# Column scores of two heads in one bank pair, with one exponential for both, once the row maxima are done

## The chip, the cores and the metric

The kernel runs on one core of one Trainium2 chip. The metric is device time in microseconds. Shown of the kernel before are three runs, with a median of 933.51 us (931.16 to 935.1), and one profiled execution, which took 931.65 us.

The core has a matrix engine (TensorE, PE in the profile), which multiplies out of SBUF and writes into PSUM, and four more engines with queues of their own: VectorE (DVE), ScalarE (ACT), GpSimd (POOL) and SyncE (SP), which here only issues DMAs. Each engine works through its own queue in order; they wait for one another by semaphores. PSUM has eight banks, and one bank holds 512 float32 columns on 128 partitions.

## The reference, cut to what matters

Input x is 2 x 2048 x 256. It is normalised by rows, and three things are added up: x itself, attention over the normalised rows, and a linear map of them that stands for a Fourier transform, a sparse product and the inverse transform.

```python
xn = layernorm(x)                                  # rows of 256
q = rope((xn @ wq).reshape(B, S, 16, 16))          # 16 heads of 16
k = rope((xn @ wk).reshape(B, S, 4, 16))           # 4 key heads, each used by 4 query heads
v = (xn @ wv).reshape(B, S, 4, 16)
scores = einsum('bshd,bthd->bhst', q, k) / 4       # causal: t <= s
out = softmax(scores) @ v
y = x + out @ wo + real(ifft(fft(xn) @ w)) + bias
```

All is float32. The head size is 16, so the 2 x 16 x 2048 x 2048 scores, half of them masked, are by far the most work.

## The kernel before, in words

The sequence is cut in blocks of 512 rows (SB), four in each of the two batches, eight blocks n in all. A unit u = (n, g) is one block of query rows with four of the 16 heads. There are 32 units, and the last, 31, belongs to the last block. Queries and keys are split in three bfloat16 parts each and stacked along the contraction (112 rows, and 3 more for the maximum), so that bfloat16 products give float32 scores.

Each unit passes two stages.

- *Row scores* (`maxima`, from line 593): scores with query rows on the partitions, only to find each row's maximum. Two heads (`head(0)`, `head(1)`) write the two banks of one tile `sm` of 2 x 512 columns from the pool `ps_s`; one VectorE maximum at line 636 reads both. The pool has two such tiles: four banks. `parts` then splits the negative maximum in three bfloat16 parts, and `spread` turns them (tile `ps_m`) and copies them (tile `mt`) into the last three rows of the stacked queries (lines 671 to 678, the last a DMA that ScalarE issues).
- *Column scores* (`scores`, line 691): scores with keys on the partitions, 128 at a time. A step is one such group of 128 keys for the four heads. Each head writes its own bank `st` of the pool `ps_st` (three banks), with the maximum already subtracted through the three extra rows. ScalarE then takes the exponential into half of an SBUF tile `es`, which holds a pair of heads (line 726). On the four steps of the diagonal the first columns drop out: 512, 384, 256 and 128 columns are left. There GpSimd masks the triangle of the pair (line 729).

`values` (line 744) multiplies the four exponentials of a step with v into the one bank `av`, at line 757; a column of ones beside v gives the sum of the exponentials. At the end of a unit `take` copies `av` into `avs` (line 768). For most units the division is done by DMA and GpSimd; for the last two it goes through TensorE (`divide`, line 819, tile `ps_a`) and `turn_back` (line 839). `output` (line 872) multiplies with `wo_sb` and the spectral matrix `mff` into a bank `po`, also from `ps_st`; the last block's outputs are begun early, without their last term, and finished at the end.

The order is written out by a planner, the loop from line 1069 on. It keeps a clock per engine, and prices for each piece (`use`, line 114; `through_bank`, line 143: TensorE fills a bank, another engine empties it). Among the pieces that could start it picks one: B is the next head's column scores, V the next step's values, A the next row scores, S a spread, F and M other pieces with and without a due time. The pieces of all queues are issued in the order in which it picks them. `ring` and `used` count the buffers of each pool, so that it knows when one comes free. `a_done` counts the row maxima issued, of `a_list` in all. TensorE's chain of work is L155 (`product`, one score or weight product as four quarters of 32 partitions), L757 (values), and L631 and L627 (row scores on the diagonal, with their mask).

Of the kernel before, what the change touches and what calls it, by code (L numbers as in the profile page):

```python
# [10 lines left out]
F32 = mybir.dt.float32  # L11
BF16 = mybir.dt.bfloat16
AF = mybir.ActivationFunctionType
# [4 lines left out]
P = 128  # L18
# [5 lines left out]
def tile_attn_plus_spectral_ffn(  # L24
# [29 lines left out]
    nc = tc.nc  # L54

    _, S, D = x.shape
# [8 lines left out]
    SB = 512  # L65
    NI = SB // P
    NJ = S // SB
    NK = D // P
    SCALE = DH ** -0.5
# [6 lines left out]
    ES = 8  # L76
# [3 lines left out]
    at_block = {bj: n for n, bj in enumerate(blocks)}  # L80
# [4 lines left out]
    ps_st = ctx.enter_context(tc.tile_pool(name="ps_st", bufs=3, space=PSUM))  # L85
    ps_s = ctx.enter_context(tc.tile_pool(name="ps_s", bufs=2, space=PSUM))
# [6 lines left out]
    ring, used = {}, {}  # L93
# [6 lines left out]
    def take_slot(tag):  # L100
        used[tag] += 1
        return used[tag] - 1
# [11 lines left out]
    def use(eng, us, needs=(), gives=()):  # L114
        clock[eng] = max(clock[eng], ready(needs)) + us
        for k in gives:
            there[k] = clock[eng] + LATE[eng]
# [25 lines left out]
    def through_bank(us, needs, eng, eng_us, gives, eng_needs=()):  # L143

        k = take_slot("st")
        use("pe", us, (*needs, ("st", k - ring["st"])), [("ps", k)])
        use(eng, eng_us, (("ps", k), *eng_needs), [("st", k), *gives])
# [220 lines left out]
    xnT, va, kst, qst = {}, {}, {}, {}  # L368
# [319 lines left out]

    es, av, es_slot = {}, {}, {}

    def scores(u, t, h):
        n, g = units[u]
        b, j = blocks[n]
        kb = kst[at_block[b, t // NI]]
        kc = (t % NI) * P
        lo = max(0, t - j * NI) * P
        pr, e = divmod(h, 2)
        if e == 0:
            es[u, t, pr] = work.tile([P, 2, SB], F32, tag="es", bufs=ES, name=f"es{u}_{t}_{pr}")
            es_slot[u, t, pr] = take_slot("es")  # L700
        ps = ps_st.tile([P, SB], F32, tag="st", name=f"st{u}_{t}_{h}")
        keys, rows = kb[0:KA, h, kc : kc + P], qst[n, g][0:KA, h, :]
        wd = SB - lo
        through_bank(
            (wd + 32 * (lo > 0 or t == 0 == j)) * 4.28e-4,
            [("mt", n, g), ("kst", at_block[b, t // NI])],
            "act", 0.06 + wd * 8.4e-4, [("es", u, t, pr)],
            [("es", es_slot[u, t, pr] - ES)],
        )
        diagonal = t >= j * NI  # L710
        if diagonal and j == 0:


            for q in range(0, P, QD):
                to, at = ps[q : q + QD, :], lo + q
                nc.tensor.matmul(  # L716
                    to[:, lo : at + QD], ident_h[:, q : q + QD], mask_t[:, : q + QD],
                    start=True, stop=True, skip_group_check=True,
                )
                nc.tensor.matmul(  # L720
                    to[:, at:], keys[:, q : q + QD], rows[:, at:],
                    start=False, stop=True, skip_group_check=True,
                )
        else:
            product(ps[:, lo:], keys, rows[:, lo:], True, True)
        nc.scalar.activation(es[u, t, pr][:, e, lo:], ps[:, lo:], AF.Exp, scale=SCALE)  # L726
        if diagonal and j > 0 and e == 1:

            nc.gpsimd.affine_select(  # L729
                out=es[u, t, pr][:, :, lo : lo + P], in_=es[u, t, pr][:, :, lo : lo + P],  # L730
                pattern=[[0, 2], [1, P]], compare_op=ALU.is_ge, fill=0.0, base=0,
                channel_multiplier=-1,
            )
            use("pool", 0.38, [("es", u, t, pr)], [("es", u, t, pr)])
# [173 lines left out]
    a_list, a_from, a_cols = [], [], [0]  # L908
# [13 lines left out]
    for at in range(NS - 1, -1, -1):  # L922
        u, t = steps[at]
        j = blocks[units[u][0]][1]
# [18 lines left out]
    k = take_slot("st")  # L943
# [70 lines left out]
    for u, (n, g) in enumerate(units):  # L1014
        end = first[u + 1]
        c, f = divmod(g, 2)
# [39 lines left out]
    streams.append(last_outs)  # L1056

    b_next, v_next, a_done, spread_next = 0, 0, 0, 0
    half = False
    SECOND = {"qst2": ("qst", 1), "raw2": ("raw", 1)}  # L1060

# [7 lines left out]
    while True:  # L1069
        now = b_next // NKV  # L1070
        pe = clock["pe"]
        choices = []

        if now < NS:
            u, t = steps[now]
            h = b_next % NKV
            n, g = units[u]
            at = start_of(
                "pe", [("mt", n, g), ("kst", at_block[blocks[n][0], t // NI])],
                ["st"] + ["es"] * (h % 2 == 0),  # L1080
            )
            if at is not None:
                choices.append((at, "B", None))

        if v_next < NS and v_next < now:
            at = start_of("pe", values_need(*steps[v_next]))
            if at is not None:
                choices.append((at, "V", None))

        if a_done < len(a_list):  # L1090
            at = pe if half else start_of("pe", a_list[a_done][2], ["s"])
            if at is not None and a_done < due[min(now + 1, NS)] + WINDOW:
                choices.append((at, "A", None))
        if spread_next < len(units) and ("np", *units[spread_next]) in there:
            at = start_of("pe", [("np", *units[spread_next])], ["st"])
            if at is not None:
                choices.append((at, "S", None))
        others = []
        for s in streams:
            if s and (s[0][0] <= now or now >= NS):  # L1100
                since, by, eng, needs, rings, what = s[0]
                at = start_of(eng, needs, rings)
                if at is None:
                    continue
                if eng == "pe":
                    choices.append((at, "F" if by <= now else "M", s))
                else:

                    if by <= now and ready(wants(needs, rings)) <= clock[eng] < pe + 1:
                        at = min(at, pe)  # L1110
                    others.append((at, s))
        limit = max(pe, min((c[0] for c in choices), default=1e9))
        if others and min(others, key=lambda c: c[0])[0] <= limit:
            soonest = min(others, key=lambda c: c[0])
            eng = soonest[1][0][2]
            s = min(
                (c for c in others if c[0] <= soonest[0] + 0.1 and c[1][0][2] == eng),
                key=lambda c: c[1][0][1],
            )[1]
            s.pop(0)[-1]()  # L1120
            continue
        if not choices:
            break
        soon = {}
        for c in choices:
            if c[0] <= pe + 0.05 and (c[1] not in soon or c[0] < soon[c[1]][0]):
                soon[c[1]] = c
        act, dve = clock["act"] - pe, clock["dve"] - pe
        lag = now - v_next
        late = a_done < due[min(now, NS)]  # L1130
        if not soon:
            pick = min(choices, key=lambda c: (c[0], "AFSBVM".index(c[1])))
        elif half and "A" in soon:
            pick = soon["A"]
        elif "S" in soon:
            pick = soon["S"]
        elif late and "A" in soon:
            pick = soon["A"]
        elif "F" in soon:
            pick = soon["F"]  # L1140
        elif "B" in soon and (act <= dve or "A" not in soon):
            pick = soon["B"]
        elif "A" in soon:
            pick = soon["A"]
        elif "V" in soon and lag > 1:
            pick = soon["V"]
        else:
            pick = soon["M"] if "M" in soon else soon["V"]
        kind = pick[1]
        if kind == "B":  # L1150
            scores(*steps[now], b_next % NKV)
            b_next += 1
            u, t = steps[now]
            if b_next % NKV == 0 and first[u + 1] == now + 1:
                n, g = units[u]
                there["qst", 2 + NG * n + g] = clock["pe"]
        elif kind == "V":
            values(*steps[v_next])
            v_next += 1
            u = steps[v_next - 1][0]  # L1160
            if first[u + 1] == v_next:
                take(u)
        elif kind == "A":
            one, two, needs, parts = a_list[a_done]
            (two if half else one)()
            if half:
                a_done += 1
                if parts:
                    parts()
            half = not half  # L1170
        elif kind == "S":
            made[spread_next][2]()
            spread_next += 1
        else:
            pick[2].pop(0)[-1]()
# [51 lines left out]
```

## Time and profile before

| What | us |
|---|---|
| median of 3 runs | 933.51 (931.16 to 935.1) |
| the profiled execution | 931.65 |
| its span, first to last instruction | 929.9 |
| TensorE busy | 906.8 |
| VectorE busy | 748.5 |
| ScalarE busy | 657.1 |
| GpSimd busy | 370.1 |
| exponentials at line 726, 1280 of them | 592.3 |
| maxima at line 636, 640 of them | 649.3 |

Busy time is the time that an engine's instructions cover; a matmul's length includes the filling of the array, so TensorE's share is an upper bound. Durations of single instructions are in ns, all else in us. An idle time has the name of the instruction that ended it behind an arrow. Views used here are the page of the whole execution, the groups of instructions of one engine (busy, mean length, idle before), busy time by stretches, the timeline of an engine (equal neighbours merged; start, length) and the chain of waits, which goes back from the last instruction to what each step waited for.

The last row maximum is issued on VectorE at 869.9; unit 30 is then in its eleventh step of sixteen.

### The profile page before, as it was taken

Reading aid. Unit: us, or ns where it says so; the run is one execution under the profiler, and the core shown is the slowest. Engines: PE = TensorE matmul, PEld = TensorE weight load, DVE = VectorE, ACT = ScalarE, POOL = GpSimd, SP = SyncE. Lnnn points to the kernel's source line nnn. Section 1 sums busy time; section 2 is a strip of 40 time slices with the busy share of each in tenths; the row PEclk is TensorE's granted clock in tenths of the full one; section 3 lists DMA queues with packets and bytes.
Section 4 is the critical chain, followed back from the end, with each engine's and each line's share of the span. In section 5 each row is a group of like instructions: output and inputs, shape, how many; then the busy total and the mean of one; then the engine's idle time right before and its main releaser. Section 6 shows DMA issues by size and latency. Waiting matters only on the chain.

```text
span 929.9 us, 39029 instructions
## 1 busy us (share of the span) xinstructions
PE 906.8 (98%) x17324; PEld 500.6 (54%) x17324; DVE 748.5 (80%) x1056; ACT 657.1 (71%) x1418; POOL 370.1 (40%) x556
## 2 busy tenths in 40 slices
PE   8999899999999999999999999999999999999996
PEld 5666665655555555555555554555455555545433
DVE  7877697789789996998986999979789987898401
ACT  3266565587657784888856778858687886778784
POOL 7398666825672424822337420302562021102201
PEclk9999899999999999999999999999999999999999
DMA  5435723341244011340002500010142000100000
GB/s 169 114 92 152 200 76 108 94 131 37 67 123 119 27 38 39 106 128 26 19 22 84 150 27 14 27 59 15 44 121 62 14 15 27 59 3 26 15 1 24
DMA packets 41993, 62.14 MB, mean 67 GB/s; under 512 B 8840, under 2 KB 32120, under 8 KB 41824
## 3 DMA queue, kind: packets, MB, share of 16 engines
q1 hardware_dynamic: 32400, 41.18, 16.5%
q0 software_dynamic: 8128, 17.69, 5.9%
q8 instruction: 135, 2.21, 1.0%
q10 hardware_dynamic: 1296, 0.79, 0.3%
q14 instruction: 34, 0.28, 0.1%
HBM read 32.75 MB, written 18.40 MB: 55 GB/s over the span
## 4 chain that ended last, share of the span: by engine, by line
PE 88%; DVE 5%; ACT 3%; issue 1%; DMA 1%; POOL 1%; ACTq 0%; POOLq 0%; DVEq 0%
PE av L757 24%; PE st L155 23%; PE sm L155 17%; PE sm L631 7%; PE po L155 6%; PE ps_q L155 4%; ACT es L726 2%; DVE mx L636 2%; PE sm L627 2%; PE st L720 2%; PE ps_x L411 1%; PE st L716 1%; PE ps_m L671 0%; DMA xt<-in_L_attn_x_dram 0%; PE ps_sw L155 0%
## 5 line engine op out<-in xcount | busy, mean ns | idle before, releaser
L726 ACT ACTIVATE es<-st 128x512 f32<-128x512 f32 (+3 forms) x1280 | 592.3, 542 | 189.3 <-PE st L155 154.1
L636 DVE TENSOR_REDUCE mx<-sm 128x2 f32<-128x1024 f32 (+3 forms) x640 | 649.3, 1058 | 88.7 <-PE sm L631 45.9
L155 PE MATMUL st<-qst,kst 115*32 115x512 bf16 (+3 forms) x4608 | 353.2, 354 | 4.7 <-ACT es L726 3.5
L757 PE MATMUL av<-es,va 128*32 128x512 f32 (+3 forms) x2560 | 299.6, 530 | 0.9 <-POOL es L729 0.5
L155 PEld LDWEIGHTS <-kst 115*32 115x32 bf16 x4608 | 162.1, 95 | 144.6 <-issue 68.3
L155 PE MATMUL sm<-kst,qst 112*32 112x512 bf16 x3072 | 239.0, 379 | 0.1
L729 POOL TENSOR_SCALAR_AFFINE_SELECT es<-es 128x256 f32<-128x256 f32 x192 | 76.7, 407 | 277.2 <-ACT es L726 274.5
L155 PEld LDWEIGHTS <-qst 112*32 112x32 bf16 x3072 | 95.9, 96 | 93.1 <-issue 64.7
L631 PE MATMUL sm<-kst,qst 112*32 112x32 bf16 (+15 forms) x2048 | 122.6, 282 | 0.6 <-DMA qst<-part 0.6
L627 PE MATMUL sm<-mask,ident_h 128*32 128x64 bf16 (+3 forms) x2048 | 100.3, 201 | 1.1 <-DVE mx L636 0.9
L757 PEld LDWEIGHTS av<-es,va 128*32 128x32 f32 x2560 | 84.9, 110 | 28.2 <-issue 2.7
L631 PEld LDWEIGHTS <-qst 112*32 112x32 bf16 x2048 | 66.5, 97 | 34.0 <-issue 20.1
L627 PEld LDWEIGHTS <-ident_h 128*32 128x32 bf16 x2048 | 66.2, 96 | 32.9 <-issue 25.9
L883 DVE TENSOR_TENSOR xr<-po,xr 128x256 f32<-128x256 f32 x36 | 15.3, 424 | 53.7 <-PE po L155 51.7
L780 POOL DMA_DIRECT2D res<-avs x30 | 18.2, 606 | 83.3 <-ACT avs L768 81.0
L155 PE MATMUL ps_q<-xnT,wp 128*32 128x512 f32 x384 | 44.7, 593 | 0.2 <-ACT xnT L414 0.2
L427 ACT COPY raw<-ps_q 128x512 f32<-128x512 f32 x24 | 14.1, 586 | 34.6 <-PE ps_q L155 34.6
L720 PE MATMUL st<-qst,kst 115*32 115x480 bf16 (+15 forms) x512 | 37.2, 288 | 0.7 <-issue 0.7
L518 POOL TENSOR_TENSOR ra<-raw,cs 128x512 f32<-128x512 f32 (+1 forms) x21 | 27.4, 1305 | 24.2 <-ACT raw L427 23.0
L716 PE MATMUL st<-mask_t,ident_h 128*32 128x128 bf16 (+3 forms) x512 | 31.4, 205 | 4.4 <-issue 3.2
L155 PE MATMUL po<-wo_sb,attT 128*32 128x256 f32 x512 | 34.4, 379 | 0.7 <-ACT attT L846 0.7
L155 PE MATMUL po<-mff,xnT 128*32 128x256 f32 x512 | 34.4, 380 | 0.0
(106 smaller groups left out, 603.2 us busy)
## 6 DMA issues: line engine op xcount, KB each, us to landing
qst<-run SPq DMA_DIRECT2D x62, 128.0 KB
res<-avs POOLq DMA_DIRECT2D x30, 256.0 KB, 3.0
run<-part SPq DMA_DIRECT2D x31, 192.0 KB
qst<-run SPq DMA_DIRECT2D x31, 192.0 KB
xt<-in_L_attn_x_dram SPq DMA_DIRECT2D x8, 512.0 KB
xr<-in_L_attn_x_dram SPq DMA_DIRECT2D x16, 256.0 KB
out_dram<-xr SPq DMA_DIRECT2D x16, 256.0 KB
sw<-raw SPq DMA_DIRECT2D x60, 64.0 KB
```

Of the source, the lines that this page charges most:

```text
L155: nc.tensor.matmul(to[q : q + QD], lhsT[:, q : q + QD], rhs, start=start, stop=stop)
L518: e.tensor_tensor(ra[c][:r], raw[c][:r], cs[j][:r, 0, :], ALU.mult)
L627: nc.tensor.matmul(to[:, at:wd], ident_h[:, q : q + QD], mask[:, q:], start=True, stop=True, skip_group_check=True,)
L631: nc.tensor.matmul(to[:, : at + QD], rows[:, q : q + QD], keys[:, : at + QD], start=False, stop=True, skip_group_check=True,)
L636: nc.vector.tensor_reduce(t["mx"][:, i, 2 * pr : 2 * pr + 2, k], ps[0][:, :, :wd], AX.X, ALU.max)
L716: nc.tensor.matmul(to[:, lo : at + QD], ident_h[:, q : q + QD], mask_t[:, : q + QD], start=True, stop=True, skip_group_check=True,)
L720: nc.tensor.matmul(to[:, at:], keys[:, q : q + QD], rows[:, at:], start=False, stop=True, skip_group_check=True,)
L726: nc.scalar.activation(es[u, t, pr][:, e, lo:], ps[:, lo:], AF.Exp, scale=SCALE)
L729: nc.gpsimd.affine_select(out=es[u, t, pr][:, :, lo : lo + P], in_=es[u, t, pr][:, :, lo : lo + P], pattern=[[0, 2], [1, P]], compare_op=A ...
L757: nc.tensor.matmul(av[u][QD * h : QD * (h + 1), lo:], va[at_block[b, t // NI]][:, t % NI, h, :], es[u, t, h // 2][:, h % 2, lo:], start=(t ...
L780: nc.gpsimd.dma_start(out=res[n, c][f], in_=avs[u])
L883: nc.vector.tensor_tensor(xr[n, r][:, e, :], po, xr[n, r][:, e, :], ALU.add)
```

## The change

While row scores are still to come, everything is as before. Once all are issued (`all_rows_done`, evaluated when a pair of heads begins), a pair's column scores take one tile of two banks from `ps_s` in place of two banks of `ps_st`. The first head of the pair issues only its matmuls, and the second head's are followed by one exponential over both. The planner's prices follow: one ScalarE piece of twice the width, with the fixed part once, and the ring "s" in place of "st".

```diff
+    wide = {}
     def scores(u, t, h):
...
             es_slot[u, t, pr] = take_slot("es")
+            wide[pr] = None
+            if all_rows_done():
+                wide[pr] = ps_s.tile([P, 2, SB], F32, tag="s", name=f"sp{u}_{t}_{pr}")
+                wide["slot", pr] = take_slot("s")
-        ps = ps_st.tile([P, SB], F32, tag="st", name=f"st{u}_{t}_{h}")
+        if wide[pr] is None:
+            ps = ps_st.tile([P, SB], F32, tag="st", name=f"st{u}_{t}_{h}")
+        else:
+            ps = wide[pr][:, e, :]
...
+            k = wide["slot", pr]
+            use("pe", pe_us, [*needs, ("s", k - ring["s"])], [("pair", k)])
+            if e == 1:
+                use("act", 0.06 + 2 * wd * 8.4e-4, [("pair", k), *free],
+                    [("s", k), ("es", u, t, pr)])
...
-        nc.scalar.activation(es[u, t, pr][:, e, lo:], ps[:, lo:], AF.Exp, scale=SCALE)
+        if wide[pr] is None:
+            nc.scalar.activation(es[u, t, pr][:, e, lo:], ps[:, lo:], AF.Exp, scale=SCALE)
+        elif e == 1:
+            nc.scalar.activation(
+                es[u, t, pr][:, :, lo:], wide[pr][:, :, lo:], AF.Exp, scale=SCALE
+            )
...
+    def all_rows_done():
+        return a_done == len(a_list)
...
-                ["st"] + ["es"] * (h % 2 == 0),
+                ["es", "s" if all_rows_done() else "st"] if h % 2 == 0
+                else ["st"] * (wide[h // 2] is None),
```

More of the change, by code (lines that the diff above doesn't have):

```diff
@@ L700, in scores @@
             es_slot[u, t, pr] = take_slot("es")
-        ps = ps_st.tile([P, SB], F32, tag="st", name=f"st{u}_{t}_{h}")
+            wide[pr] = None
[6 more added lines that the diff above has]
+            ps = wide[pr][:, e, :]
         keys, rows = kb[0:KA, h, kc : kc + P], qst[n, g][0:KA, h, :]
         wd = SB - lo
[L704 to L709, printed above, removed]
+        pe_us = (wd + 32 * (lo > 0 or t == 0 == j)) * 4.28e-4
+        needs = [("mt", n, g), ("kst", at_block[b, t // NI])]
+        free = [("es", es_slot[u, t, pr] - ES)]
+        if wide[pr] is None:
+            through_bank(
+                pe_us, needs, "act", 0.06 + wd * 8.4e-4, [("es", u, t, pr)], free
+            )
+        else:
+            k = wide["slot", pr]
[3 more added lines that the diff above has]
+                    [("s", k), ("es", u, t, pr)])
         diagonal = t >= j * NI
@@ L725, in scores @@
             product(ps[:, lo:], keys, rows[:, lo:], True, True)
-        nc.scalar.activation(es[u, t, pr][:, e, lo:], ps[:, lo:], AF.Exp, scale=SCALE)
+        if wide[pr] is None:
+            nc.scalar.activation(es[u, t, pr][:, e, lo:], ps[:, lo:], AF.Exp, scale=SCALE)
+        elif e == 1:
+            nc.scalar.activation(
+                es[u, t, pr][:, :, lo:], wide[pr][:, :, lo:], AF.Exp, scale=SCALE
+            )
         if diagonal and j > 0 and e == 1:
```

## The prediction

> **What bounds the kernel now.** I read the page first, for the bound of the whole, then busy time cut at the points where this change acts, then ScalarE's timeline and the chain inside those cuts.
>
> ```profile
> span 929.9 us, 39029 instructions
> PE 906.8 (98%) x17324; PEld 500.6 (54%) x17324; DVE 748.5 (80%) x1056; ACT 657.1 (71%) x1418; POOL 370.1 (40%) x556
> PE 88%; DVE 5%; ACT 3%; issue 1%; DMA 1%; POOL 1%; ACTq 0%; POOLq 0%; DVEq 0%
> ```
>
> TensorE is busy almost throughout, so over the whole kernel an edit that saves ScalarE time would be worth nothing. But the edit acts only after the last row maximum. In VectorE's timeline (start, length) its last rows are
>
> ```profile
> 868.77 2.36 DVE L636 TENSOR_REDUCE mx<-sm 128x2 f32<-128x1024 f32 x2 [0.36 <-PE sm L631]
> ```
>
> and on TensorE the last row-score pair ends at 869.4. From there to the end is 6.5% of the span. Busy time in cuts of it (columns: stretch, length, PE, PEld, DVE, ACT, POOL, then granted clock):
>
> ```profile
> 869.40:881.60 12.20, 11.04 (x156) 4.64 (x145) 2.82 (x9) 9.55 (x23) 2.27 (x6) 1.00 0.01 2
> 881.60:888.70 7.10, 6.75 (x92) 2.83 (x88) 0.00 (x0) 6.92 (x15) 3.40 (x5) 1.00 0.01 2
> 888.70:895.10 6.40, 5.72 (x74) 2.23 (x77) 0.68 (x2) 5.70 (x12) 0.00 (x0) 1.00 0.00 0
> 895.10:914.10 19.00, 17.95 (x268) 8.23 (x264) 1.28 (x3) 15.48 (x30) 0.41 (x1) 1.00 0.01 2
> 914.10:921.20 7.10, 5.44 (x87) 2.78 (x76) 0.42 (x1) 4.33 (x13) 2.85 (x7) 1.00 0.01 3
> ```
>
> Neither engine is full here: busy PE is modelled and counts the fill of the pipe. I count its real work by the pitch of the chain below: 0.215 us for one head's scores at 512 columns, 0.86 for one step's values, 1.30 for an output group, the narrow steps in proportion. That gives 9.5, 5.6, 5.2, 17.3 and 3.5 us for the five stretches, 41 of 51.8 us: about 10.7 us of TensorE idle. The granted clock is 1.00, so no share of it is a slow clock. The chain of waits (start, length) shows where the idle comes from, in a step of the last unit:
>
> ```profile
> 893.80 0.40 PE st L155 x4
> 894.20 0.86 PE av L757 x8
> 895.06 0.24 PE st L155 x4
> 895.32 0.61 ACT es L726
> 895.97 0.40 PE st L155 x4
> ```
>
> One step takes 895.97 - 893.80 = 2.17 us, though TensorE has only 4 x 0.215 + 0.86 = 1.72 of work. The fourth head's scores need a bank; of the three, the oldest is freed by an exponential that could start only after the values had passed. So a loop through three banks sets the end, not an engine. ScalarE's own rate (start, length of the run):
>
> ```profile
> 889.20 1.09 ACT L726 ACTIVATE es<-st 128x512 f32<-128x512 f32 x2 [0.38 <-PE st L155]
> 918.38 0.61 ACT L726 ACTIVATE es<-st 128x128 f32<-128x128 f32 x3 [0.47 <-PE st L155]
> L726 ACT ACTIVATE es<-st 128x512 f32<-128x512 f32 x896 | 470.9, 607 | 125.2 <-PE st L155 108.5 <-PE st L720 4.7 <-ACT mt L677 2.4
> L726 ACT ACTIVATE es<-st 128x128 f32<-128x128 f32 x128 | 29.6, 277 | 24.0 <-PE st L155 14.4 <-PE st L720 8.6
> ```
>
> A lone one lasts 0.60; two in a row end after 1.09, so the start-to-start pitch is 0.48. At 128 columns (0.61 - 0.28) / 2 = 0.165. Slope 0.82 ns per column, fixed part 0.06 us. In length (607 and 277 ns) slope 0.86 ns, fixed part 0.167.
>
> **The change, part by part.**
>
> *Moved, outside the end:* nothing. The order of instructions on TensorE is the same up to 869.4, and on VectorE, GpSimd and SyncE to the end of the program; no DMA moves on SP's or POOL's queue. The gain or loss is all in the last 61 us. The 8.7 us from 921.2 (last attention block turned back, last outputs, output DMA) keep their instructions and only start at another time.
>
> *Removed and added on ScalarE:* 86 exponentials become 43 (one and a half steps of unit 30 at full width, then its four diagonal steps, then all of unit 31). No row shows a 1024-column exponential. From the rows above its pitch is 0.06 + 1024 x 0.82 ns = 0.90 against 2 x 0.48 = 0.96, its length 0.167 + 1024 x 0.86 ns = 1.05. Bounds: 0.84 (no fixed part) and 0.96 (nothing saved), and dearer if reading two banks costs extra; the nearest row for that is VectorE's maximum, which reads both banks of such a pair, 1.22 us for 1024 elements and 0.42 for 256, so 1.04 ns an element with no visible surcharge. I take 0.90. The Trainium skill, ScalarE: Activation LUTs, What ACT_TABLE_LOAD costs, gives 186 ns + 0.833 ns per element and an overlap of about 93 ns, an estimate of 0.52 where the row has 0.48, and 0.946 for the pair. With 0.946 the sum below would lose about 0.9 us; the row decides. Saving 0.06 x 43 = 2.6 us of ScalarE time would by itself be worth little, since ScalarE isn't full.
>
> *Changed hand-off:* the column scores leave the three single banks for the two pairs (four banks) that the row scores used. The first pair waits for the last maxima but one (870.0), the second for the last (871.1); the planned order puts a step of values before each, so TensorE doesn't stand. The single banks then serve only the mt transposes, the outputs and the division, so outputs no longer wait behind scores. Against it: TensorE gets a bank back only after 1.05 us instead of 0.60, and the first head's result waits for the second. The Trainium skill, Perfetto Trace Analysis, Optimizing Scalar/DVE Operations, says that where ScalarE is not saturated but causes bubbles, breaking instructions up may let work complete sooner. That is this case (5.70 busy of 6.40) and speaks against merging. So the loop has to be worked out. In the new order TensorE runs [pair 1 of step t][values][pair 0 of t+1][pair 1 of t+1 ...]. From the start of a held-up pair 1: 0.43 + 0.86 + 0.215 to the second head of the next pair 0, 0.45 from that head's start to its exponential (894.87 to 895.32 before), 0.90 to the next exponential, 1.05 to its end, 0.05 to restart: 3.96 us, and that spans two steps: 1.98 per step against 2.17. If the page's rule held, the loop would still close once a step, with 0.215 more for the second head and 0.45 more of length: 2.17 + 0.67 = 2.84, and over the six steps before the outputs 4 us slower. By the rows it shrinks by 0.19 a step, since two pairs hold four heads in flight and the loop closes once in two steps. I take the rows.
>
> *The outputs:* before, four steps in a row hold one output group each, 3.03 us a step (TensorE-bound), and the three and a half ahead of them run at 2.17. In the new order the outputs stand one to two steps, from step 6 on: per two steps TensorE has 2 x 1.72 + 1.30 = 4.74 of work, more than the 3.96 of the loop and the 3.6 of ScalarE. So from step 6 to step 13 TensorE is full: 7 x 0.86 scores + 6 x 0.86 values + 4 x 1.30 = 16.4 us against 19.06 in the trace. Of these 2.6, 1.7 is idle removed; 0.86 is one step of values that falls after step 13, where TensorE has idle left (3.6 us of 7.1).
>
> *Sum.* I wrote each group of both planned orders out with those prices: a group starts at the later of the end of the one before it and the release of its buffers. Start of the scores of unit 31:
>
> ```
>                       old, worked   old, trace   new, worked
> step 0                   881.2        881.6        880.4
> step 3                   888.2        888.7        886.9
> step 6                   894.5        895.1        892.7
> step 13                  913.6        914.1        909.2
> last division (ps_a)     920.1        921.2        915.6
> ```
>
> The same rule on the old order is 1.1 us short of the trace, most of it at narrow steps, in hand-offs of single banks. Compared like with like the gain is 4.5; if the new order has none of that shortfall it is 5.6. It has half as many hand-offs, so I take a third of the difference: **4.9 us**. The profiled execution took 931.65 (929.9 span and 1.7 around it): 926.8 for it. The median shown is 933.51, 1.9 higher; the prediction is made for that: **928.6**.
>
> **Rivals.**
>
> *A dearer wide exponential.* Each 0.05 us on a pair costs about 1.0 us in the same working, since step loop, diagonal steps and drain carry it and only the output stretch hides it. Between 0.93 and 1.0 the gain is 2 to 4: 930 to 931.5. For: the page's 0.946. Against: rows of four widths on one line.
>
> *Slower: release in pairs becomes the new wait.* Place: the free steps and the diagonals. If the exponential across two banks costs 0.21 more than 0.90, the loop is 2.17 again and the gain is gone; at 0.43 more it is 4.7 us slower, 938. For: bubbles of ScalarE already set the pace. Against: VectorE's two-bank rows.
>
> *More than worked out:* if the saved fixed part is nearer the 0.167 of the lengths than 0.06, pairs go at 0.84 and all hand-offs shrink: 6 to 7.5 us, 926 to 927.5.
>
> *Nothing happens,* because the drain or GpSimd's masks on the diagonal set the end: 933.5. Against: those masks take 0.41 each, and their number and order stay.
>
> **How the numbers follow.** No change measures to about 0.5%, 4.7 us, here. Main case (4.2 to 5.7 us, 927.8 to 929.3) 0.64, of which 0.43 above 4.7; more than worked out 0.14; dearer 0.11; nothing 0.03; slower 0.08. Faster 0.43 + 0.14 = 0.57, same 0.21 + 0.11 + 0.03 = 0.35, slower 0.08. Range 926.5 to 932: main, most of "more" and of "dearer".
>
> **What would show it.** Right: 43 exponentials of two heads, 1024 columns with a pitch near 0.90 and 1.05 long; free steps near 2.0 us; steps 6 to 13 near 16.5 with TensorE at the work's pitch; the last division 4.5 to 5.6 earlier; nothing moved before 869. Wrong: a pitch above 1.0, free steps at 2.17 or more with TensorE waiting for ScalarE, or a new wait where the score pairs meet the last maxima.

## The result

The changed kernel took 926.44 us in the median of seven runs (924.64 to 929.84), the kernel before 931.16 in seven (928.63 to 935.1). The ratio is 0.9947, with a 95% interval of 0.9922 to 0.9972. Of the median of before, that is 4.9 us less, with 2.6 to 7.3 as its interval; the two medians differ by 4.72. That is the forecast gain, in part by chance, for the stretch that the change touches lost less, as shown below. The time itself lies 0.06 us below the low end of the range, since the forecast was made for a base of 933.51 that seven runs, the three shown among them, put at 931.16.

The profiled execution took 926.44, with a span of 924.7 against 929.9. The head of its page, and the chain by engine:

```profile
span 924.7 us, 38985 instructions
PE 904.6 (98%) x17324; PEld 500.5 (54%) x17324; DVE 748.0 (81%) x1056; ACT 653.7 (71%) x1375; POOL 370.1 (40%) x556
PE 89%; DVE 5%; ACT 3%; issue 1%; DMA 1%; POOL 1%; ACTq 0%; SPq 0%; DVEq 0%; POOLq 0%
```

43 ScalarE instructions are gone (1418 to 1375), and 3.4 us of its busy time; the other engines have the same number of instructions. On TensorE's timeline (start, length) the last row scores and the last division mark the ends of the tail that the change can touch. Of the kernel before:

```profile
869.24 0.40 PE L631 MATMUL sm<-kst,qst 112*32 112x480 bf16 x4
921.20 0.66 PE L827 MATMUL ps_a<-ident,avs 128*128 128x128 f32 x4 [0.71 <-ACT avs L768]
```

and of the changed one:

```profile
868.46 0.40 PE L631 MATMUL sm<-kst,qst 112*32 112x480 bf16 x4
916.03 0.66 PE L850 MATMUL ps_a<-ident,avs 128*128 128x128 f32 x4 [0.69 <-ACT avs L791]
```

From the one to the other it is 51.96 us before and 47.57 after: the tail lost **4.39 us**. The other 0.8 us of the 5.2 between the two spans lie ahead of it (869.24 against 868.46), where both programs are the same. From here on "tail" means this stretch; it is a far finer measure than the median, for in three executions of the changed program it took 47.57, 47.58 and 47.57. Of the kernel before there is one trace.

Busy time of the changed kernel in the stretches that answer to those shown of before (each about 0.8 us earlier in this execution, and cut at the same steps; columns as there):

```profile
868.50:880.10 11.60, 10.81 (x160) 5.46 (x153) 2.94 (x9) 9.10 (x14) 2.31 (x6) 1.00 0.01 2
880.10:886.70 6.60, 6.17 (x88) 2.58 (x90) 0.68 (x2) 6.13 (x8) 3.37 (x5) 1.00 0.01 2
886.70:892.50 5.80, 5.50 (x76) 2.13 (x72) 0.00 (x0) 5.29 (x7) 0.00 (x0) 1.00 0.00 0
892.50:909.10 16.60, 16.60 (x260) 8.17 (x259) 1.41 (x4) 13.41 (x14) 0.23 (x1) 1.00 0.01 2
909.10:916.00 6.90, 6.17 (x95) 2.87 (x84) 0.29 (x1) 4.94 (x8) 3.00 (x8) 1.00 0.01 2
```

The output stretch, fourth, was 19.0 us and is 16.6, with TensorE full; the free steps, third, were 6.4 and are 5.8. So over half of the gain falls where the outputs are. There the change acts in two ways at once: the loop is shorter, and the planner now puts an output group into every other step from step 6 on, where before the last four had one each, with TensorE full, and the steps ahead of them ran at the loop's 2.17. What these places for the outputs would give with the old banks no run here shows. The chain of waits through two free steps of the changed kernel:

```profile
887.41 0.46 ACT es L747
...
888.33 1.03 ACT es L747
...
889.40 0.61 PE sp L155 x8
890.01 0.86 PE av L780 x8
890.87 0.97 PE sp L155 x16
```

and ScalarE's timeline there:

```profile
887.41 3.77 ACT L747 ACTIVATE es<-sp 128x1024 f32<-128x1024 f32 x4 [0.27 <-PE sp L155]
891.41 1.94 ACT L747 ACTIVATE es<-sp 128x1024 f32<-128x1024 f32 x2 [0.23 <-PE sp L155]
```

This is the worked-out loop: a held-up pair waits for the second of two exponentials, and passes through two steps until the next hold-up. One full round fits in before the outputs begin. The exponentials that begin a round start at 887.41 and 891.41: 4.00 us for two steps, 3.96 in the working, 4.34 before. Four exponentials in a row give the pitch, (3.77 - 1.03) / 3 = 0.91 against 0.90 worked out, and each lasts 1.03 against 1.05.

### The profile page after: what moved, and what is told of

Its sections match the earlier page's. It is cut to its first block, busy times and chain, and to the rows that moved or that the text cites. A ratio compares the mean times of both kernels' runs of the same rounds, so it can differ in the third digit from the quotient of the medians.

```text
span 924.7 us, 38985 instructions
## 1 busy us (share of the span) xinstructions
PE 904.6 (98%) x17324; PEld 500.5 (54%) x17324; DVE 748.0 (81%) x1056; ACT 653.7 (71%) x1375; POOL 370.1 (40%) x556
## 3 DMA queue, kind: packets, MB, share of 16 engines
q8 instruction: 135, 2.21, 1.0%
## 4 chain that ended last, share of the span: by engine, by line
PE 89%; DVE 5%; ACT 3%; issue 1%; DMA 1%; POOL 1%; ACTq 0%; SPq 0%; DVEq 0%; POOLq 0%
PE av L780 24%; PE st L155 22%; PE sm L155 17%; PE sm L631 7%; PE po L155 6%; PE ps_q L155 4%; DVE mx L636 2%; PE sp L155 2%; PE sm L627 2%; PE st L738 2%; ACT es L745 1%; PE ps_x L411 1%; PE st L734 1%; ACT es L747 1%; PE ps_m L671 0%
## 5 line engine op out<-in xcount | busy, mean ns | idle before, releaser
L745 ACT ACTIVATE es<-st 128x512 f32<-128x512 f32 (+3 forms) x1194 | 552.4, 543 | 179.2 <-PE st L155 145.6
L155 PE MATMUL st<-qst,kst 115*32 115x512 bf16 (+3 forms) x4264 | 327.2, 354 | 1.1 <-ACT es L745 0.4
L627 PE MATMUL sm<-mask,ident_h 128*32 128x128 bf16 (+3 forms) x2048 | 100.2, 201 | 1.8 <-DVE mx L636 1.0
L747 ACT ACTIVATE es<-sp 128x1024 f32<-128x1024 f32 (+3 forms) x43 | 36.6, 907 | 7.6 <-PE sp L155 7.4
```

The costliest lines, as they stand in the source:

```text
L155: nc.tensor.matmul(to[q : q + QD], lhsT[:, q : q + QD], rhs, start=start, stop=stop)
L627: nc.tensor.matmul(to[:, at:wd], ident_h[:, q : q + QD], mask[:, q:], start=True, stop=True, skip_group_check=True,)
L747: nc.scalar.activation(es[u, t, pr][:, :, lo:], wide[pr][:, :, lo:], AF.Exp, scale=SCALE)
```

## The experiments

The question was what makes the 4.4 us. Theory A, that of the prediction: the hand-off of banks (four heads in flight instead of three, released in a slower loop). Theory B: the overhead of 43 exponentials that are saved. The expectations for the first repeat, head by head, four exponentials and five banks count the tail from the first work after the last row scores, 0.19 us later than here (51.8 and 47.4); those of the others count as here.

### The changed kernel again

No edit.

> The changed kernel once more, beside the others. The tail, from the start of the first values after the last row scores to the start of the last division (ps_a), was 51.8 us before (869.4 to 921.2) and 47.4 us in the changed kernel (868.6 to 916.0). Both theories expect 47.4 again, within 0.2, and 4.4 us less than the kernel before in the median; what differs from that between executions should lie in the first 115 us, where the two traces differed by up to 1 us either way.

> The changed kernel beside it: tail 47.6, ratio to the kernel before 0.994 to 0.995.

Tails of 47.58 and 47.57 us. Medians of 924.46 (six runs) and 925.66 (ten), ratios of 0.9938 (0.9918 to 0.9957) and 0.9942 (0.9922 to 0.9962). The gains by the ratio, 5.8 and 5.4 us, are above the tail's 4.39, which both intervals hold. So the changed kernel's tail repeats to 0.01 us, and what its executions differ by lies elsewhere.

### Unmerged, head by head

```diff
-        elif e == 1:
-            nc.scalar.activation(es[u, t, pr][:, :, lo:], wide[pr][:, :, lo:], AF.Exp, scale=SCALE)
+        else:
+            nc.scalar.activation(es[u, t, pr][:, e, lo:], wide[pr][:, e, lo:], AF.Exp, scale=SCALE)
```

> Same bank pairs, same order of every queue, but two exponentials of one head each instead of one over both. Theory A (the gain is the hand-off: four heads' banks in flight instead of three, released in two steps' loop): ScalarE pays 0.96 instead of 0.90 a pair but the first head's exponential starts 0.2 earlier, so the tail is within 0.3 us of the changed kernel's, 47.2 to 47.7. Theory B (the gain is the saved overhead of 43 exponentials): the gain is lost, the tail is 50 us or more, near the 51.8 of before.

Six executions took 973.64 to 998.97 us, 986.23 in the median; the ratio, 1.0499 (1.0455 to 1.0543), is that of the three shortest. The trace is of the longest, and its tail is 116.2 us. Neither theory had that, and it decides nothing between them, for the edit did more than it was meant to. TensorE's timeline of this kernel:

```profile
871.21 0.43 PE L155 MATMUL sp<-qst,kst 115*32 115x512 bf16 x4
872.39 0.40 PE L155 MATMUL sp<-qst,kst 115*32 115x512 bf16 x4 [0.74 <-ACT es L747]
872.60 1.04 PE L780 MATMUL av<-es,va 128*32 128x512 f32 x8
873.46 0.40 PE L155 MATMUL sp<-qst,kst 115*32 115x512 bf16 x4
874.62 0.61 PE L155 MATMUL sp<-qst,kst 115*32 115x512 bf16 x8 [0.76 <-ACT es L747]
```

The second head's matmuls wait for the first head's exponential, though that reads the other bank: the pair is one tile, and the wait seems to be kept for the tile. In total (us, times, longest):

```profile
PE sp L155 <- ACT es L747: 30.2, 43, 1.0
```

One wait in each of the 43 pairs makes 30.2 of the 68.6 us by which this tail is longer than the changed kernel's. The rest is told under the hardware below.

### Four exponentials per pair

```diff
         elif e == 1:
-            nc.scalar.activation(es[u, t, pr][:, :, lo:], wide[pr][:, :, lo:], AF.Exp, scale=SCALE)
+            for f in range(2):
+                for c in range(lo, SB, wd // 2):
+                    nc.scalar.activation(es[u, t, pr][:, f, c : c + wd // 2],
+                                         wide[pr][:, f, c : c + wd // 2], AF.Exp, scale=SCALE)
```

> Same bank pairs and order, four exponentials of half a head each, all issued after the second head's matmuls: ScalarE pays 4 x 0.27 = 1.08 per full pair instead of 0.90. It measures what a dearer exponential costs. Theory A with its loop: about 2.1 us more than the changed kernel in the tail, 49.5, still below the 51.8 of before. By the prediction's 1.0 us per 0.05 it would be 3.6 more, 51.0. Theory B: 51.8 or more, as 43 x 0.18 = 7.7 us of ScalarE time come on top.

Tail 51.06, 3.5 us longer, and 931.14 us in twelve runs, ratio 1.0004 (0.999 to 1.0018). This is close to the prediction's rule (1.0 us per 0.05 on a pair, 3.6), not to the 2.1 of the expectation, which had let the first half start before the second head was done. ScalarE's timeline shows why: TensorE no longer interrupts it,

```profile
885.10 11.29 ACT L749 ACTIVATE es<-sp 128x256 f32<-128x256 f32 x40
```

so ScalarE has become what sets the pace in the free steps. Still the tail is 0.9 us shorter than before the change, with twice as many exponentials as then. Theory B, which has 51.8 or more there, falls as the whole cause.

### Unmerged, both after the second head

```diff
         elif e == 1:
-            nc.scalar.activation(es[u, t, pr][:, :, lo:], wide[pr][:, :, lo:], AF.Exp, scale=SCALE)
+            for f in range(2):
+                nc.scalar.activation(es[u, t, pr][:, f, lo:], wide[pr][:, f, lo:], AF.Exp, scale=SCALE)
```

> Two exponentials of one head each, both issued after the second head's matmuls, in the pairs and the order of the changed kernel: the merging alone is undone, and no matmul waits for the first of the two. ScalarE pays 0.96 instead of 0.90 a full pair. Theory A with the measured slope of the four-way split (3.5 us for 0.18, so 1.0 per 0.05): the tail is 47.6 + 1.0 to 1.2 = 48.6 to 48.8, so about 3.3 us of the gain stay without any merging. Theory B (the saved overhead is the gain): 51.5 or more.

Tail 48.85, median 927.14 of eight runs, ratio 0.9952 (0.9935 to 0.997). This undoes the merging alone, with both exponentials still held back to the second head. Of the 4.39 us, 3.11 stay without it, and 1.28 are the merging's.

### Five single banks, nothing merged

```diff
+    turn_of = [0]
+    def tail_tag():
+        return "st" if turn_of[0] % 5 < 3 else "s"
...
-        ps = ps_st.tile([P, SB], F32, tag="st", name=f"st{u}_{t}_{h}")
+        spare = all_rows_done() and tail_tag() == "s"
+        if all_rows_done():
+            turn_of[0] += 1
+        if spare:
+            ps = ps_s.tile([P, 2, SB], F32, tag="s", name=f"sp{u}_{t}_{h}")[:, 0, :]
+        else:
+            ps = ps_st.tile([P, SB], F32, tag="st", name=f"st{u}_{t}_{h}")
...
-                ["st"] + ["es"] * (h % 2 == 0),
+                [tail_tag() if all_rows_done() else "st"] + ["es"] * (h % 2 == 0),
```

> The kernel before, with single exponentials of one head, but once the row scores are done the column scores take five single banks in turn: the three of before and the first bank of each of the two row-score tiles. No exponential is merged and no head waits for another. Theory A: the loop through the banks is gone, ScalarE's 1.92 per step is the floor in free steps, the tail is 46 to 47 us, 0.5 to 1.3 below the changed kernel. Theory B: no overhead is saved, so it stays at 51 to 52.

Tail 46.21, 5.75 us less than before and 1.36 less than the changed kernel; 923.16 us in six runs, ratio 0.9914 (0.9895 to 0.9933), a gain of 6.2 to 9.8, more than the tail's. ScalarE's timeline in the free steps:

```profile
886.64 1.61 ACT L741 ACTIVATE es<-st 128x512 f32<-128x512 f32 x3
888.08 1.16 ACT L741 ACTIVATE es<-sp 128x512 f32<-128x512 f32 x2
889.03 1.67 ACT L741 ACTIVATE es<-st 128x512 f32<-128x512 f32 x3
```

Five heads take 889.03 - 886.64 = 2.39 us, 0.48 each, without a pause: ScalarE's own rate, 1.91 a step. Deeper banks with the old exponentials beat merged ones in two pairs. That settles it for A as the main cause; the merging's own part is the 1.28.

### Seven banks: one pair, two singles a step

```diff
-            if all_rows_done():
+            if all_rows_done() and pr == 0:
                 wide[pr] = ps_s.tile([P, 2, SB], F32, tag="s", name=f"sp{u}_{t}_{pr}")
...
-                ["es", "s" if all_rows_done() else "st"] if h % 2 == 0
+                ["es", "s" if all_rows_done() and h == 0 else "st"] if h % 2 == 0
```

> Once the row scores are done, heads 0 and 1 share a bank pair and one exponential, heads 2 and 3 use the three single banks with one exponential each: seven banks in turn instead of four. Theory A: the loop through the banks is gone, ScalarE needs 0.90 + 0.96 = 1.86 in a free step, TensorE 1.72. Tail 45.4 to 45.8, 1.8 to 2.2 below the changed kernel and 0.5 to 0.8 below the five single banks; about 923 us where the changed kernel takes 924.5. Theory B: half of the exponentials are unmerged again, so the tail is near 49.5.

> Seven banks alone: tail 45.4, 2.2 below the changed kernel; in the median 1 to 2 us below it.

Tail 45.36 both times, 2.21 below the changed kernel. Medians 924.68 (about 923 was expected) and 925.17 of six runs each, ratios 0.9925 (0.9904 to 0.9947) and 0.9942 (0.9922 to 0.9962). The second was timed beside the changed kernel, which took 925.66: 0.5 us, less than expected and less than the tails say, and inside the noise of the rest. In the chain of waits of a free step there is no engine but TensorE left, and a step takes 889.87 - 888.15 = 1.72 us, its bare work:

```profile
888.15 0.22 PE st L155 x4
888.37 0.43 PE sp L155 x8
888.80 0.22 PE st L155 x4
889.01 0.86 PE av L780 x8
889.87 0.22 PE st L155 x4
```

ScalarE is no faster than was worked out. Its wide exponentials there start 1.86 us apart,

```profile
889.36 1.11 ACT L747 ACTIVATE es<-sp 128x1024 f32<-128x1024 f32 x1
891.22 1.15 ACT L747 ACTIVATE es<-sp 128x1024 f32<-128x1024 f32 x1
```

so it falls 0.14 behind in each step, and seven banks are enough to carry that to the outputs, where it catches up. With five, TensorE had to keep to ScalarE's 1.91.

### Outputs in two parts, over the whole last unit

```diff
-                    last_outs.append((end - 10, end - 6 + i, "pe", output_needs(n, i, whole[:-1]), ["st"],
-                        lambda n=n, i=i: output(n, i, whole[:-1])))
+                    for terms, at in ((whole[:NK], end - 17), (whole[NK:-1], end - 9)):
+                        at += 2 * i
+                        last_outs.append((at, at + 4, "pe", output_needs(n, i, terms), ["st"],
+                            lambda n=n, i=i, terms=terms: output(n, i, terms)))
```

(with the residual's load eight steps earlier, and the pieces in order of their steps.)

> The changed kernel with the last block's early output groups cut in two (the two spectral terms, then the first attention term) and offered from the last unit's start on, to fill TensorE's idle in the free steps. No theory doubts the mechanism; if the free steps' idle (0.26 us in each of some six) is what remains there, the tail is 46.6 to 47.0, 0.6 to 1.0 below the changed kernel. If the groups only push the scores back, it stays at 47.6 or above.

> Both of the last two together. With seven banks TensorE has less idle left to fill: worked out 0.4 above the seven banks alone, 46.0, because two output pieces land near the end; 45.0 if their place at the end costs nothing.

> Seven banks and the outputs cut in two once more, timed in rounds beside the changed kernel on one chip. The tail should be 45.9 us as in its first look, 1.7 below the changed kernel's 47.6; the medians should differ by as much, give or take the 1 to 2 us by which executions of one program differ before the tail and after it.

On the changed kernel: tail 46.63, 0.94 less; 925.69 us in four runs, ratio 0.9937 (0.9915 to 0.9959). Together with seven banks: 45.87 and 45.88, 0.5 worse than seven banks alone, as worked out, since little idle is left to fill and two pieces land at the end. It took 922.5 us in its single run, and 923.79 in the median of six, ratio 0.9928 (0.9905 to 0.9952), when timed beside the changed kernel's 925.66.

So three versions beat the changed kernel's tail by 1.4 to 2.2 us (five banks, seven banks, seven with the outputs spread). Which of them is best in the median these runs can't tell.

## Why the prediction was right, and where it was wrong

The bound was read rightly: no engine, but a loop through three banks, in the last 6.5% of the span. The experiments without merging (3.1 and 5.75 us of gain) show that.

**What failed is the last step of the sum: "the prediction is made for that: 928.6".** The gain of 4.9 was taken from the median shown, 933.51, a median of three. Seven runs gave 931.16, and later ones on three other occasions 930.96 (seventeen runs), 932.07 and 931.07 (fifteen each). That term was 2.4 us too high. From 931.16 the same gain would have given 926.3, against 926.44. The same text had 926.8 for the profiled execution, from its own base of 931.65; it took 926.44, with 0.8 us of help from ahead of the tail. And the range was built from the cases of the gain alone; the base, whose own runs spread by 0.4% in the times shown, had no place in it. With 2 us for it the low end would have been below 925.

The size of the tail's gain was off by less. "Compared like with like the gain is 4.5": it is 4.39. "It has half as many hand-offs, so I take a third of the difference: 4.9" was wrong: the shortfall of the working did not shrink. Moved by the 0.78 us by which this execution is early, the new trace has the scores of step 0 at 880.9, of step 3 at 887.5, of step 6 at 893.3, of step 13 at 909.9 and the last division at 916.8, against 880.4, 886.9, 892.7, 909.2 and 915.6 worked out. It is 0.5, 0.6, 0.6, 0.7 and 1.2 us short, where the old order was 0.4, 0.5, 0.6, 0.5 and 1.1 short. The narrow steps at the end fell short by about as much in both. That the profiled spans differ by 5.2, near the 4.9, is luck: 0.8 us of it come from elsewhere.

The other steps, as they stood:

- *Pitch 0.90, length 1.05:* 0.91 and 1.03. The row was nearer than the 0.946 worked out from the Trainium skill, ScalarE: Activation LUTs, What ACT_TABLE_LOAD costs. No surcharge for reading two banks shows, so the "dearer" and the "slower" rival both fall.
- *"Saving 0.06 x 43 = 2.6 us of ScalarE time would by itself be worth little":* too low. The merging alone is worth 1.28 us in these banks, as the unmerged pair shows. The prediction's own slope said so: 1.0 us per 0.05 on a pair.
- *That slope:* undoing the merging puts about 0.05 on a pair (two starts of 0.48 against 0.91) and cost 1.28. Four exponentials start 0.28 apart (the 40 in the row above), which is 1.11 a pair, 0.20 more, and cost 3.5. So 0.9 to 1.3 per 0.05.
- *The rule to break instructions up* (the Trainium skill, Perfetto Trace Analysis, Optimizing Scalar/DVE Operations), which spoke against the change: breaking the exponential up lost in all three forms tried here, by 1.28, 3.5 and 69 us in the tail, the last through waits on the shared tile and a halved clock. The bubbles came from too few banks. Where these were added instead, the bubbles went, with unmerged exponentials (five banks).
- *Free step 1.98:* 2.00. *Steps 6 to 13 in 16.4:* 16.6 with TensorE full.
- *"Nothing moved before 869"* holds for the program. The 0.8 us there come from the first 118 us, where the last section finds the spread between executions.

## What to carry to other kernels

When an engine has idle at a steady period, follow the chain around one period before counting instruction overhead: if it passes through a buffer's release, more buffers in flight are worth more than cheaper instructions, and a merged instruction can pay mainly because it brings other buffers along. When a change acts on one stretch, measure that stretch between two fixed instructions in the trace: here it repeats to 0.01 us, where three medians of six to ten runs of the changed kernel lie 2.0 apart. And a forecast for a whole kernel's time needs a range for the base as well as for the gain.

## What the runs showed of the hardware

**Short waits can halve TensorE's clock, and it need not come back.** In the head-by-head kernel TensorE stood for up to 1.0 us in each pair. Busy time of that kernel in three stretches (length, PE, PEld, DVE, ACT, POOL, granted clock, DMA):

```profile
870.50:876.80 6.30, 3.83 (x52) 1.44 (x45) 2.64 (x9) 3.57 (x8) 0.00 (x0) 1.00 0.00 0
876.80:907.00 30.20, 21.92 (x169) 6.68 (x160) 0.00 (x0) 13.21 (x28) 5.70 (x10) 0.50 0.01 1
907.00:986.30 79.30, 59.16 (x440) 19.00 (x436) 2.38 (x6) 29.88 (x56) 3.26 (x8) 0.52 0.00 1
```

After 6 us with TensorE busy 61% of the time the clock falls to half, at 876.8, and stays there through nearly all of the tail, although at half clock TensorE is busy for 73 to 75% of it. Of the 68.6 us the 43 waits are 30.2; the other 38 are put down to the half clock by subtraction. The six executions fit this: the shortest, 973.64, has a mean granted clock of 0.975, the longest 0.941. The unmerged pair that is held back to the second head has the same exponentials in the same banks, without the waits, and its clock stays at 1.00 through the tail.

What decides can be narrowed from the traces. Their clock records change only in steps of 3.41 us. Of this kernel, three such steps (the first and the third end in a change):

```profile
873.40:876.80 3.40, 1.68 (x28) 0.74 (x24) 0.00 (x0) 1.86 (x5) 0.00 (x0) 0.99 0.00 0
883.60:887.00 3.40, 2.81 (x23) 0.61 (x13) 0.00 (x0) 1.28 (x3) 0.41 (x1) 0.50 0.00 0
941.60:945.00 3.40, 2.94 (x28) 1.37 (x31) 0.00 (x0) 1.01 (x2) 0.00 (x0) 0.50 0.00 0
```

and one of seven banks with the outputs in two parts (its single run), with no change after it:

```profile
910.30:913.70 3.40, 1.75 (x29) 1.02 (x22) 1.11 (x3) 0.59 (x1) 0.15 (x1) 1.00 0.00 0
```

At full clock, TensorE busy for 1.68 of 3.40 us was too little, and 1.75 was enough. In all 13 traces, after their first 20 us, the clock fell after each step with half or less and after none with more; in the first 20 us it fell after three with 57 to 65%. Busy time is modelled, so the limit holds for this measure of it. From half clock the way back asks for more: steps of up to 2.81 of 3.40 stayed at half, 2.94 was enough, with one exception at the end of this kernel (81%). The 73 to 75% at which this kernel ran lie below that. The longest single gap in the tail is 0.97 us. The Trainium skill, TensorE: Matmul & The Clock Gate, Part 1: The HAM clock gate, puts the fall after an idle window of about 3.4 us; the length of the step agrees, but here a window with half of it idle, in small pieces, was enough.

**The spread between executions of one program has a place.** Up to the tail, the kernel before and the first repeat of the changed one run the same instructions. From the maximum at 159.4 us on, the repeat is 4.75 us ahead, and stays so to within 0.02 until the tail. 1.2 of these have come together in small pieces by 100 us, and the rest arises in one place. Of the kernel before:

```profile
100.00:103.50 3.50, 3.23 (x114) 2.29 (x107) 2.43 (x9) 2.41 (x8) 2.32 (x4) 1.00 1.01 199
103.50:106.70 3.20, 0.00 (x1) 0.00 (x1) 0.94 (x1) 0.00 (x0) 3.12 (x4) 0.82 0.56 177
106.70:112.40 5.70, 5.70 (x109) 4.54 (x112) 2.68 (x3) 2.17 (x6) 2.74 (x3) 0.50 0.81 215
```

and of the repeat:

```profile
100.00:103.50 3.50, 2.78 (x115) 2.23 (x111) 2.25 (x3) 1.94 (x8) 3.48 (x5) 1.00 1.04 216
103.50:106.70 3.20, 3.20 (x111) 2.57 (x98) 2.74 (x3) 2.38 (x5) 3.12 (x4) 1.00 0.65 199
106.70:112.40 5.70, 4.88 (x157) 3.15 (x152) 5.07 (x13) 3.89 (x12) 4.26 (x8) 1.00 0.96 282
```

In the one TensorE stands for 3.2 us, just after the DMA engines were full (a share of 1.01, then 0.56), and works at half clock from 105.6 on for 6.8 us; in the other neither happens. The profile names no cause of the standstill ("issue"), and none was tried. It sorts the traces: in the five with a half clock about there the last row scores start at 868.5 to 870.9, in the eight without it at 864.5 to 869.3, and all but one of these by 867.6. At the other end the repeat lost 1.4 us: its clock was halved from 914.4 to 917.8, under the last outputs, which took 3.4 us instead of 1.9, so that from the last division to the end of the span it was 10.1 us instead of 8.7. These two places are as large as most effects measured here, so a median of three runs is a poor base. Whether the three shown had them is not on record; but of 47 later runs of the kernel before, the 13 with a mean granted clock of 0.998 or more have a median of 930.04 us, the 32 with 0.996 or less one of 931.77.
